# A convolution and attention block on one core: loads for the first image's Strassen sums issued earlier, and a division moved behind the last addition

## The chip, the cores and the metric

The kernel runs on one core of a Trainium2 chip. The metric is the device time of one execution in microseconds. The kernel before takes 2338.26 us, the median of three runs (2337.59 to 2338.87).

## The reference

Eight images of 512 channels and 32 x 32 pixels, all in float32. Each goes through a group norm, then through this block, and is added to the result:

```python
t = cbs(x, cv1_w, cv1_bn, 0)               # 1x1 convolution 512 -> 512, batch norm, silu
ys = [t[:, :C], t[:, C:]]                  # two halves of C = 256 channels
for i in range(N):                         # N = 2 bottlenecks
    yi = ys[-1]
    z = cbs(yi, m_cv1_w[i], m_cv1_bn[i], 1)                    # 3x3 convolution
    z = bot_attention(z, m_qkv_w[i], m_rw[i], m_rh[i])         # 4 heads of 64, 1024 positions
    z = jax.nn.silu(bn_eval(conv2d(z, m_cv2_w[i], 0), m_cv2_bn[i]))
    ys.append(yi + z)
return cbs(jnp.concatenate(ys, axis=1), cv2_w, cv2_bn, 0)      # 1x1 convolution 1024 -> 512
```

The attention takes q, k and v from a 1x1 convolution, adds a position term to k, and divides the exponentials of the scaled products by their sums.

## The kernel before, in words

**The stages of an image.** A Python loop over the eight images is unrolled. For each image: `conv3x3` of the first bottleneck (with the inputs transformed by `tiles_in` and the weights by `make_u`), `attention_fast`, the 1x1 convolution `m2` (L938), then the same again for the second bottleneck, then `cv2`. Parts of the next image's group norm and `cv1` and of this image's `cv2` are put inside the attention calls, to fill TensorE.

**Strassen.** From the second image on, `cv1` (L1084) and the projections q, k, v (L582, L586) are computed by Strassen's scheme on 2 x 2 blocks; `cv2` (L972) is for all images but the last. The scheme needs four sums of weight blocks each. They are made once, during the second attention of the first image, and put to DRAM, from which the later images load them: `make_ws` (for `cv2`), `make_sq(0)` and `make_sq(1)` (for the projections of the two bottlenecks) and `make_sw` (for `cv1`). `make_sw` first loads the weights of `cv1` as two halves of 512 KB (`w1_half`, L241, on SyncE's queue), makes the sums s1 to s4 on VectorE (L246 to L249) and stores them on GpSimd's queue (L251). `make_ws` finds its weights on the chip, and so does `make_sq`.

**Attention.** `attention_fast` walks over four groups: a group is a pair of heads and a half of the queries. A group has eight blocks of keys, taken in four pairs. For a pair, TensorE makes the products of q and k (L689), ScalarE takes the exponentials (L693, one for each block), VectorE adds them up in `acc` (L707 for the first pair, L709 otherwise), and TensorE multiplies them with v, one pair behind (L723). At a group's end ScalarE and VectorE bring the two halves of the result from PSUM to `ao` (L730, L731).

**The division.** TensorE sums `acc` over the partitions (`sums`, L741). The row of sums goes to DRAM (L748) and back in another shape (L778), VectorE takes the reciprocal (L785), and it goes to DRAM (L787) and comes back spread over the partitions as `rs` (L789). Then VectorE multiplies `ao` with it (`scale`, L797). The sums of group g are taken in group g + 1, its `rs` is made in the third pair of group g + 1, and its `scale` stands in the second pair of group g + 2. The last two groups are different. The fourth group's sums go a shorter way (`last_sums`, L759: two copies of the PSUM tile, an addition L834 and a reciprocal L835 on VectorE). The third group's `scale` is called at the end of `attention_fast`, between `last_sums` and L834.

**What orders the work.** The tile framework orders each engine's queue at compile time from the order of the program and from what it expects to be ready. `with tc.issue_after(ins)` puts the instructions of the block behind `ins` on its engine. A dictionary `behind` hands functions to `attention_fast`, which calls them at set places: -1 is behind the projections, g behind the first pair of v products of group g, (g, p) behind pair p of group g, `NG` = 4 behind the last pair, and `NG + 1` behind `last_sums`. All places but -1 are inside `issue_after(added.ins)`, where `added` is the latest addition to `acc`.

**The first image's second attention** has in `behind`: 0 `make_ws`, 1 the Strassen closures of `cv2` and the loads of the next transformed 3 x 3 weights (L332), 2 `make_sq(0)`, (2, 2) `make_sq(1)`, 3 `make_sw`, 4 the first product of `cv2` (`part1`: the sums `t1` on VectorE, L997, and 16 matmuls from the first image's `y` and `ypad`), 5 the second product (`part2`, from `t1`). That second product goes to the one PSUM buffer of tag `av`, which L731 frees.

**Buffers.** The `w1_half` tiles, the tiles of `make_sq` and the image tiles share the four buffers of tag `x`. The tiles of `make_sw` and the residual tiles `x_res` (loaded by GpSimd's queue, L1016) share the two of tag `xr`.

Of the kernel before, what the change touches and what calls it, by code (L numbers as in the profile page):

```python
# [61 lines left out]
def kernel(  # L62
# [47 lines left out]
    def ring(shape, name):  # L110
        return const.tile(shape, F32, tag="u", name=name, bufs=5)
# [6 lines left out]
    def load_w2(n=2):  # L118
        nk = (2 + N) * NM // 2
        ws = [ring([P, nk, C2], f"w2_{i}") for i in range(n)]  # L120
        for i, w in enumerate(ws):
            nc.sync.dma_start(w, cv2_w[ts(i, nk * P), :].rearrange("(k p) o -> p k o", p=P))
        return ws
# [90 lines left out]
    def block_qkv(n, o, i):  # L214
        return qkv_sb[:, n, i].rearrange("p (w c o) -> p c w o", w=3, c=NM)[:, o]
# [3 lines left out]
    def make_sq(n):  # L219
        (a11, a12), (a21, a22) = ([block_qkv(n, o, i) for i in range(2)] for o in range(2))  # L220
        parts = [act.tile([P, 2, 3, P], F32, tag="x", name="sq_new", bufs=NX) for _ in range(2)]
        s1, s2, s3, s4 = (t[:, j] for t in parts for j in range(2))
        nc.vector.tensor_tensor(s1, a21, a22, ALU.add)
        nc.vector.tensor_tensor(s2, s1, a11, ALU.subtract)
        nc.vector.tensor_tensor(s3, a11, a21, ALU.subtract)
        nc.vector.tensor_tensor(s4, a12, s2, ALU.subtract)
        for h, t in enumerate(parts):
            nc.gpsimd.dma_start(sq_dram[n][:, 2 * h : 2 * h + 2], t)
# [5 lines left out]

    sw_dram = tc.dram_tile([P, 4, NX // 2, C], F32, name="sw")

    def make_sw():
        halves = []
        for o in range(2):
            a = act.tile([P, NX, C], F32, tag="x", name="w1_half", bufs=NX)  # L240
            nc.sync.dma_start(a, cv1_w[:, ts(o, C)].rearrange("(k p) o -> p k o", p=P))  # L241
            halves.append((a[:, : NX // 2], a[:, NX // 2 :]))
        (a11, a12), (a21, a22) = halves
        parts = [act.tile([P, 2, NX // 2, C], F32, tag="xr", name="sw_new", bufs=2) for _ in range(2)]
        s1, s2, s3, s4 = (t[:, j] for t in parts for j in range(2))
        nc.vector.tensor_tensor(s1, a21, a22, ALU.add)  # L246
        nc.vector.tensor_tensor(s2, s1, a11, ALU.subtract)
        nc.vector.tensor_tensor(s3, a11, a21, ALU.subtract)
        nc.vector.tensor_tensor(s4, a12, s2, ALU.subtract)  # L249
        for h, t in enumerate(parts):  # L250
            nc.gpsimd.dma_start(sw_dram[:, 2 * h : 2 * h + 2], t)  # L251
# [78 lines left out]
    def load_u(n, oc, i):  # L330
        u = new_u("u")
        nc.sync.dma_start(u, u_dram[n][oc][i])  # L332
        return u
# [13 lines left out]
    def stages(act, small, ps_big, ps_av, n_pt):  # L347
# [316 lines left out]
        def attention_fast(n, z, at, behind, sq=None, mid=None):  # L664
# [13 lines left out]
            def logits(pair):  # L678
                g, j0 = pair[0]
                c, half = groups[g]  # L680
                pt = act.tile([P, PAIR, 2, HALF], F32, tag="pt", name="pt", bufs=n_pt)
                pts[pair[0]] = pt
                for i, (_, j) in enumerate(pair):
                    ps = ps_big.tile([P, 2, HALF], F32, tag="big", name="l_ps")
                    for hd in range(2):
                        r = slice(hd * HD, (hd + 1) * HD)
                        for kh in range(2):
                            o = j * P + kh * HD
                            nc.tensor.matmul(  # L689
                                ps[kh * HD : (kh + 1) * HD, hd, :], kr[r, c, o : o + HD],  # L690
                                q[r, c, ts(half, HALF)], start=True, stop=True,
                            )
                    exp = nc.scalar.activation(pt[:, i], ps, AF.Exp, scale=SCALE)  # L693
                if pair is pairs[-1]:
                    with tc.issue_after(exp.ins):
                        silu_in.append(table_of(AF.Silu))
                if j0 == 0 and g == 1 and later is not None:
                    accs[g] = None
                    return exp
                return add_up(pair)  # L700

            def add_up(pair):
                g, j0 = pair[0]
                pt = pts[pair[0]]
                if j0 == 0:
                    accs[g] = act.tile([P, 2, HALF], F32, tag="acc", name="acc", bufs=2)
                    return nc.vector.tensor_tensor(accs[g], pt[:, 0], pt[:, 1], ALU.add)  # L707
                for i in range(PAIR):
                    ins = nc.vector.tensor_tensor(accs[g], accs[g], pt[:, i], ALU.add)  # L709
                return ins  # L710
# [83 lines left out]
            def scale(g, rs):  # L794
                c, half = groups[g]
                dst = ao[:, c, ts(half, HALF)]
                nc.vector.tensor_tensor(dst, dst, rs, ALU.mult)  # L797
# [5 lines left out]
            s_drams, rss, evicted = {}, {}, [None]  # L803
            for i in range(len(pairs) + 1):
                if i < len(pairs):
                    added = logits(pairs[i])
                    g, at_q = divmod(i, NQ)
# [7 lines left out]
                if i > 0:  # L815
                    g, j0 = pairs[i - 1][0]
# [3 lines left out]
                    if i < len(pairs) and accs.get(pairs[i][0][0], 0) is None:  # L820
                        with tc.issue_after(evicted[0].ins):
                            added = add_up(pairs[i])
# [5 lines left out]
            g = len(groups) - 1  # L828
            ps, rows, s_dram = last_sums(g)
            with tc.issue_after(added.ins):  # L830
                behind.get(len(groups) + 1, lambda: None)()
            scale(g - 1, rss.pop(g - 1))
            rs = act.tile([P, HALF], F32, tag="rs", name="rs", bufs=2)
            nc.vector.tensor_tensor(rs, ps[:, 1, :], rows[0], ALU.add)  # L834
            nc.vector.reciprocal(rs, rs)  # L835
# [405 lines left out]
    for b in range(B):  # L1241
# [6 lines left out]
        def u_of(n):  # L1248
            def of(oc):
                nonlocal last_load  # L1250
                if b == 0 and oc == 1:
                    if n == 0:
                        with tc.issue_after(last.ins):
                            for i in range(PAIRS):
                                make(n, oc, [i])
                    else:
                        for k in range(NM):
                            raws[n, oc, k] = load_raw(n, oc, k, "kv"[k])
                        with tc.issue_after(last.ins):
                            make(n, oc, [1])  # L1260
                got = [us.pop((oc, i)) if (oc, i) in us else load_u(n, oc, i) for i in range(PAIRS)]
                if b > 0 and oc == 1:
                    sq[n], last_load = load_sq(n)
                return got

            return of
# [20 lines left out]
        def ahead():  # L1287
            nonlocal w1, sw
            g = next(groups)
            if g > 0 or b == 0:  # L1290
                next(norm, None)
            if g == 0:
                if b > 0:
                    for i in range(PAIRS):
                        us[0, i] = load_u(1, 0, i)
                w1 = load_w1() if more else load_w2(1)
                if more and b > 0:
                    sw = load_sw()
            if b == 0:
                if g == 0:  # L1300
                    raws[1, 1, 0], raws[1, 1, 1] = load_raws_y0(1, 1)
                    make(1, 1, [2])
                    del us[1, 2]
                elif g <= NM:
                    make(1, 1, [0], [g - 1])
# [22 lines left out]
        behind = {g: ahead for g in range(NG)} | {NG: first, NG + 1: second}  # L1328
# [16 lines left out]
        with tc.issue_after(last.ins):  # L1345
            check()
        z, mid = s.conv3x3(1, vs, u_of(1))
        w2 = ws = three = stored = None
        begun = {}
        if b == 0:  # L1350
            w2 = load_w2()

        def prepare():
            nonlocal stored, ws
            stored, ws = make_ws(w2)

        def ahead():
            nonlocal w2, three
            if more:
                three = s.strassen(b, ws or load_ws(), y0, y1)  # L1360
                for i in range(PAIRS):
                    us[0, i] = load_u(0, 0, i)
            else:
                w2 = load_w2()
# [10 lines left out]
        def second():  # L1375
            if more:
                three[1]()
            else:
                ks = range(2 * NM, (1 + N) * NM)
                begun[1] = ps_av.tile([P, NH, HALF], F32, tag="av", name="ps")  # L1380
                s.cv2_products(w2, (y0, y1, y2), 1, ks, begun[1], (ks[0], (2 + N) * NM - 1))

        behind = {1: ahead, NG: first, NG + 1: second}
        if b == 0:
            behind |= {0: prepare, 2: lambda: make_sq(0), (2, 2): lambda: make_sq(1), 3: make_sw}
        if six:
            behind |= {(1, 1): six[3], (2, 1): six[4]}
        ao, check = s.attention_fast(1, z, (b * N + 1) * NM * NH, behind, sq.get(1), mid)
# [29 lines left out]
    with tc.If(held < P):  # L1418
        with ExitStack() as gs:
# [6 lines left out]
            g = stages(g_act, g_small, g_big, g_av, 3)  # L1426
# [67 lines left out]
```

## Time and profile before

| | share of the span, or us |
|---|---|
| span of the profiled run | 2337.2 us |
| TensorE busy | 98% |
| VectorE busy | 78% |
| ScalarE busy | 42% |
| GpSimd busy | 4% |
| mean granted TensorE clock | 0.996 |
| DMA traffic, mean | 100 GB/s |

The page also gives the chain of work that ended last, followed back from the last instruction. It is TensorE for 93% of the span and VectorE for 4%. A busy TensorE in this profile includes the modelled ends of pipelined matmuls, so in the timelines the distance from one start to the next is the better measure: it is 0.43 us for a matmul of 128x128 by 512.

In a timeline, a row merges equal instructions of one engine. It has the start and the length in us, the engine, the line of the kernel, the operation, output and inputs, their shapes and the count. Brackets at the end give the idle time of the engine ahead of the row and what ended it. A name ending in q, as `SPq`, is the engine's queue of issues (DMA starts); the time of such a row is that of the issue, not of the transfer.

### The profile page before, as it was taken

The numbers are of one execution on the slowest core, as the hardware profiler recorded it, in microseconds if no ns is written. First come the engines' busy times: TensorE is split into PE (matmuls) and PEld (weight loads), VectorE is DVE, ScalarE is ACT, GpSimd is POOL, SyncE is SP. The second block draws the span as 40 slices with busy tenths as digits, with TensorE's granted clock in tenths as the row PEclk, the third lists the DMA queues.
The fourth block names the chain that finished last, engine by engine and source line by source line (L and its number), as shares of the span: only waits on it lengthen the run. The fifth ranks groups of instructions, "written<-read, shape, count | busy, mean of one in ns | idle before, by whom it ended". The sixth has DMA issues, their size and how long they took to land.

```text
span 2337.2 us, 36365 instructions
## 1 busy us (share of the span) xinstructions
PE 2298.2 (98%) x14746; PEld 1162.6 (50%) x14746; DVE 1826.2 (78%) x2899; ACT 980.2 (42%) x1282; POOL 88.9 (4%) x307
## 2 busy tenths in 40 slices
PE   7999989999999999999999999999999999999998
PEld 4536336363463635536364463645536364463643
DVE  8867767878778887888778877888877888777674
ACT  1442613536245362444525445253543535335352
POOL 1000000000000000000000000000000000000001
PEclk9999999999999999999999999999999999999999
DMA  7412326031240414304152131612216031250202
GB/s 255 154 54 90 109 78 230 15 131 48 94 193 15 149 33 142 143 15 149 34 200 89 47 113 51 240 36 78 82 46 247 29 120 40 65 219 16 86 11 70
DMA packets 95280, 234.80 MB, mean 100 GB/s; under 512 B 28032, under 2 KB 50496, under 8 KB 81664
## 3 DMA queue, kind: packets, MB, share of 16 engines
q1 hardware_dynamic: 83296, 182.05, 22.9%
q0 software_dynamic: 11808, 50.34, 5.6%
q8 instruction: 118, 1.93, 0.3%
q14 instruction: 58, 0.48, 0.1%
HBM read 197.75 MB, written 34.60 MB: 99 GB/s over the span
## 4 chain that ended last, share of the span: by engine, by line
PE 93%; DVE 4%; DMA 1%; ACT 1%; issue 0%; SPq 0%; POOL 0%; DVEq 0%; ACTq 0%
PE av_ps L723 18%; PE l_ps L689 18%; PE c_ps L917 14%; PE c L972 8%; PE p_ps L582 7%; PE x_ps L1084 6%; PE c_new L972 6%; PE m_ps L938 5%; PE ps L369 5%; PE pv_ps L586 3%; PE s_ps L741 1%; PE p_ps L586 1%; DVE acc L709 1%; PE s_ps L759 1%; PE v_ps L553 1%
## 5 line engine op out<-in xcount | busy, mean ns | idle before, releaser
L693 ACT ACTIVATE pt<-l_ps 128x1024 f32<-128x1024 f32 x512 | 494.9, 1023 | 408.4 <-PE l_ps L689 385.1
L709 DVE TENSOR_TENSOR acc<-acc,pt 128x1024 f32<-128x1024 f32 x384 | 469.4, 1222 | 65.8 <-ACT pt L693 42.5
L723 PE MATMUL av_ps<-pt,vT 64*64 64x512 f32 x4096 | 485.1, 591 | 1.1 <-DVE ao L731 1.1
L689 PE MATMUL l_ps<-q,kr 64*64 64x512 f32 x4096 | 484.2, 590 | 0.0
L917 PEld LDWEIGHTS c_ps<-v_in,u 128*128 128x128 f32 x2720 | 306.3, 192 | 8.0 <-issue 6.7
L917 PE MATMUL c_ps<-v_in,u 128*128 128x128 f32 x2720 | 306.9, 275 | 1.1 <-DVE v_in L426 1.1
L723 PEld LDWEIGHTS av_ps<-pt,vT 64*64 64x64 f32 x4096 | 152.0, 133 | 277.3 <-issue 230.7
L689 PEld LDWEIGHTS l_ps<-q,kr 64*64 64x64 f32 x4096 | 153.7, 133 | 269.7 <-issue 256.2
L433 ACT COPY m<-c_ps 128x256 f32<-128x256 f32 x96 | 35.4, 369 | 227.5 <-PE c_ps L917 222.5
L972 PE MATMUL c_new<-t_in,ws 128*128 128x512 f32 x288 | 124.6, 592 | 0.0
L938 PE MATMUL m_ps<-ao,m_sb 128*128 128x512 f32 x256 | 112.7, 593 | 0.0
L707 DVE TENSOR_TENSOR acc<-pt 128x1024 f32<-128x1024 f32 x64 | 78.1, 1220 | 25.8 <-ACT pt L693 25.8
L352 ACT ACTIVATE m_kept<-m_kept,bh,sh 128x512 f32<-128x512 f32 x42 | 31.9, 806 | 146.0 <-DVE m_kept L1056 86.3
L797 DVE TENSOR_TENSOR ao<-ao,rs 128x512 f32<-128x512 f32 x64 | 44.1, 689 | 60.4 <-DMA rs<-r_dram 59.8
L972 PEld LDWEIGHTS c_new<-t_in,ws 128*128 128x128 f32 x288 | 54.7, 190 | 68.9 <-issue 66.0
L352 ACT ACTIVATE t<-m_ps,bh,sh 128x512 f32<-128x512 f32 x64 | 48.0, 775 | 84.2 <-PE m_ps L938 82.7
L582 PE MATMUL p_ps<-t_z,sq 128*128 128x512 f32 x168 | 81.3, 593 | 0.0
L938 PEld LDWEIGHTS m_ps<-ao,m_sb 128*128 128x128 f32 x256 | 48.4, 190 | 61.7 <-issue 58.4
L946 DVE TENSOR_TENSOR ylast<-t,ypad 128x512 f32<-128x512 f32 x32 | 22.0, 692 | 66.5 <-ACT t L352 66.5
L352 ACT ACTIVATE z<-z,bh,sh 128x512 f32<-128x512 f32 x64 | 48.6, 806 | 50.9 <-DVE z L462 50.9
L426 DVE TENSOR_TENSOR v_in<-w_rows 128x512 f32<-128x512 f32 x96 | 65.9, 687 | 0.0
L972 PE MATMUL c<-ypad,ws 128*128 128x512 f32 x144 | 63.8, 592 | 0.0
(252 smaller groups left out, 2976.8 us busy)
## 6 DMA issues: line engine op xcount, KB each, us to landing
u<-u SPq DMA_DIRECT2D x85, 1024.0 KB
x<-in_x_dram SPq DMA_DIRECT2D x32, 512.0 KB
x_res<-in_x_dram POOLq DMA_DIRECT2D x28, 512.0 KB, 6.8
out_dram<-m_kept POOLq DMA_DIRECT2D x28, 512.0 KB, 7.3
w<-in_cv_w_dram SPq DMA_DIRECT2D x13, 1024.0 KB
u<-u_new POOLq DMA_DIRECT2D x12, 1024.0 KB, 5.6
rs<-r_dram SPq DMA_DIRECT2D x96, 128.0 KB
ws<-s SPq DMA_DIRECT2D x24, 512.0 KB
```

The lines of the kernel that those rows point to most:

```text
L352: return nc.scalar.activation(dst, src, AF.Silu, scale=sh[:, k : k + 1], bias=bh[:, k : k + 1])
L369: nc.tensor.matmul(ps[:, half, :], w_of(k), rhs_of(k, half), start=(k == begin), stop=(k == end))
L582: nc.tensor.matmul(ps[:, o, :], w[:, o, :], rhs, start=not onto, stop=True, skip_group_check=onto)
L586: nc.tensor.matmul(v[:, ts(j, P)], rhs[:, ts(j, P)], w[:, 2, :], start=j == 0 and not onto, stop=True, skip_group_check=True,)
L689: nc.tensor.matmul(ps[kh * HD : (kh + 1) * HD, hd, :], kr[r, c, o : o + HD], q[r, c, ts(half, HALF)], start=True, stop=True,)
L693: exp = nc.scalar.activation(pt[:, i], ps, AF.Exp, scale=SCALE)
L709: ins = nc.vector.tensor_tensor(accs[g], accs[g], pt[:, i], ALU.add)
L723: nc.tensor.matmul(avs[g][hd * HD : (hd + 1) * HD, kh, :], vT[r, j, o : o + HD], pt[r, i, hd, :], start=(j == 0), stop=(j == NJ - 1),)
L917: nc.tensor.matmul(ps[:, row, col, :], us[i][:, k, row, SLOT[col], :], vs[i][:, k, row, col, :], start=(k == 0), stop=(k == NM - 1),)
L938: nc.tensor.matmul(pss[oc][:, half, :], m2_sb[:, n, k, ts(oc, P)], ao[:, k, ts(half, HALF)], start=(k == 0), stop=(k == NM - 1),)
L972: nc.tensor.matmul(ps[:, o, :], w[:, k, ts(o, P)], rhs[part][:, c, :], start=(k == 0 and not onto), stop=(k == KB - 1), skip_group_check=onto,
L1084: nc.tensor.matmul(ps[:, o, :], w[:, c, ts(o, P)], rhs[c], start=(c == 0 and not onto), stop=(c == 1), skip_group_check=onto,)
```

## The change

It has three parts, all about the work that the first image's second attention does besides its own.

- `make_sw` is split. `load_halves` issues the two loads of `cv1`'s weights behind the projections of that attention (place -1), and `make_sw` makes the sums and stores them. It is called in the second group (place 1, in `ahead`) instead of the fourth (place 3).
- `make_sq(1)` moves from pair 2 of the third group, (2, 2), to the fourth group, 3, where `make_sw` was.
- In all 16 attention calls the third group's `scale` is put behind the last addition to `acc`, by an `issue_after`. Before, only the order of the program and its inputs bound it.

The first part is meant to have the loads behind the chip's other transfers and not among those of the division, the third to keep a division whose `rs` is late from holding up the last addition, on which `last_sums` waits.

```diff
-    def make_sw():
+    def load_halves():
         halves = []
         for o in range(2):
             a = act.tile([P, NX, C], F32, tag="x", name="w1_half", bufs=NX)
             nc.sync.dma_start(a, cv1_w[:, ts(o, C)].rearrange("(k p) o -> p k o", p=P))
             halves.append((a[:, : NX // 2], a[:, NX // 2 :]))
+        return halves
+
+    def make_sw(halves):
         (a11, a12), (a21, a22) = halves
...
             with tc.issue_after(added.ins):
                 behind.get(len(groups) + 1, lambda: None)()
-            scale(g - 1, rss.pop(g - 1))
+            with tc.issue_after(added.ins):
+                scale(g - 1, rss.pop(g - 1))
             rs = act.tile([P, HALF], F32, tag="rs", name="rs", bufs=2)
...
+        def load_ahead():
+            nonlocal halves
+            halves = load_halves()
+
...
         def ahead():
             nonlocal w2, three
+            if b == 0:
+                make_sw(halves)
             if more:
                 three = s.strassen(b, ws or load_ws(), y0, y1)
...
         if b == 0:
-            behind |= {0: prepare, 2: lambda: make_sq(0), (2, 2): lambda: make_sq(1), 3: make_sw}
+            behind |= {-1: load_ahead, 0: prepare, 2: lambda: make_sq(0), 3: lambda: make_sq(1)}
```

More of the change, by code (lines that the diff above doesn't have):

```diff
@@ L1347 @@
         z, mid = s.conv3x3(1, vs, u_of(1))
-        w2 = ws = three = stored = None
+        w2 = ws = three = stored = halves = None
         begun = {}
```

## The prediction

> **What bounds the kernel now.** I read the busy table first: TensorE is busy 98% of the span, and nothing else is near it. So a change to loads and VectorE adds can only win what TensorE loses by waiting, some 39 us in all, and the next view is the list of TensorE's waits (engine, line waited for, us in total, times, longest).
>
> ```profile
> PE 2298.2 (98%) x14746; PEld 1162.6 (50%) x14746; DVE 1826.2 (78%) x2899; ACT 980.2 (42%) x1282; POOL 88.9 (4%) x307
> ```
>
> ```profile
> PE gm_ps L475 <- DVE mv L470: 11.2, 1, 11.2
> PE s_ps L759 <- DVE acc L709: 5.1, 1, 5.1
> ...
> PE c L972 <- DVE ao L731: 1.9, 1, 1.9
> ```
>
> The first is the start of the kernel, which the change does not touch. The other two occur once each in 16 attention calls. The timeline of TensorE puts both in the first image's second attention; below it stands the same stretch of the second image.
>
> ```profile
> 291.19 3.70 PE L972 MATMUL c<-y,w 128*128 128x512 f32 x8
> 294.72 3.60 PE L972 MATMUL c<-ypad,w 128*128 128x512 f32 x8
> 303.43 1.98 PE L759 MATMUL s_ps<-acc,ones 64*64 64x512 f32 x8 [5.11 <-DVE acc L709]
> 307.35 9.00 PE L972 MATMUL c<-t_in,s 128*128 128x512 f32 x16 [1.93 <-DVE ao L731]
> ```
>
> ```profile
> 584.89 3.70 PE L972 MATMUL c<-y,ws 128*128 128x512 f32 x8
> 588.43 3.60 PE L972 MATMUL c<-ypad,ws 128*128 128x512 f32 x8
> 591.96 1.09 PE L759 MATMUL s_ps<-acc,ones 64*64 64x512 f32 x8
> 592.98 7.13 PE L972 MATMUL c<-t_in,ws 128*128 128x512 f32 x16
> 599.95 6.60 PE L938 MATMUL m_ps<-ao,m_sb 128*128 128x512 f32 x15
> ```
>
> From the first `c` to the first `m_ps` the second image takes 599.95 - 584.89 = 15.06 us. In the first image `m_ps` starts at 316.19, so the same 40 matmuls take 25.00 us. The excess, 9.94 us, is three things: `s_ps` starts 12.24 instead of 7.07 us after the first `c` (5.17), the next product 3.92 instead of 1.02 us after that (2.90), `m_ps` 8.84 instead of 6.97 us after that (1.87). The last term has no wait in it: after the hole the clock is halved. By windows the granted clock is 0.86 in 298 to 302, 0.50 in 302 to 306 and 0.57 in 306 to 312, about 10.3 us at half speed.
>
> Why `s_ps` is late is in VectorE's queue of that stretch:
>
> ```profile
> 282.96 0.68 DVE L797 TENSOR_TENSOR ao<-ao,rs 128x512 f32<-128x512 f32 x1
> 286.20 0.69 DVE L246 TENSOR_TENSOR sw_new<-w_half 128x512 f32<-128x512 f32 x1 [2.55 <-DMA w_half<-in_cv_w_dram]
> ...
> 291.20 0.20 DVE L785 RECIPROCAL rc<-sums_all 128x8 f32<-128x8 f32 x1
> 291.39 1.23 DVE L709 TENSOR_TENSOR acc<-acc,pt 128x1024 f32<-128x1024 f32 x1
> 301.46 0.69 DVE L797 TENSOR_TENSOR ao<-ao,rs 128x512 f32<-128x512 f32 x1 [8.84 <-DMA rs<-r_dram]
> 302.07 1.22 DVE L709 TENSOR_TENSOR acc<-acc,pt 128x1024 f32<-128x1024 f32 x1
> ```
>
> The third group's division (L797) stands ahead of the fourth group's last addition (L709), waits 8.84 us for `rs`, and the addition, the three sums of `t_in` and the PSUM addition L731 queue behind it. TensorE waits for the last L709, then for L731. `rs` itself is late, as the SyncE queue shows:
>
> ```profile
> 277.85 1.14 SPq L241 DMA_DIRECT2D w_half<-in_cv_w_dram x2
> 281.66 0.52 SPq L748 DMA_DIRECT2D s_dram<-s_row  x1
> 286.36 0.33 SPq L778 DMA_DIRECT2D sums_all<-s_dram  x1
> 291.43 0.34 SPq L787 DMA_DIRECT2D r_dram<-rc  x1
> 294.73 1.10 SPq L789 DMA_DIRECT2D rs<-r_dram  x2
> ```
>
> The tiny `s_dram` write holds L778 for 4.70 us behind the two halves of the weights (in the first group, at 252.03, it was 1.66). The reciprocal is late behind 2.55 us of wait for `w_half` and 2.54 us of its four sums (286.20 to 288.74), and the return of `rs` takes 3.30 us to issue and 6.73 more to arrive. In the second image these are 1.41 (581.06 to 582.47) and 3.58 (582.47 to 586.05). Meanwhile two residual loads of 512 KB go out on GpSimd's queue at 292.33 and 294.83, having waited for the sums' store.
>
> [...]
>
> **The change part by part.** *The loads.* Two loads of 512 KB go to behind the projections, about 230 us, or earlier, since the SyncE queue issues nothing between 211.34 and 252.03 and the DMA share is 0.00 from 220 to 230. Before they took at most 8.35 us (277.85 to 286.20), with other transfers beside them; so they are there by 240 and are needed near 254. Nothing waits for them, and they leave the stretch that matters. Cost 0.
>
> *The four sums in the second group.* 2.54 us of VectorE behind the second pair of group 1, near 254.2. VectorE there waits for ScalarE's exponentials 1.52 + 0.77 + 1.79 = 4.08 us up to 263.5, so the sums fit and 1.54 us is left. Behind them are that group's additions, which only release exponential buffers, and the first group's reciprocal, which moves from 258.2 to about 259.3; its `rs` comes by about 265, and its L797 stands at 268.5. Cost 0. Their stores and the residual loads, which wait for them, move 25 to 30 us earlier.
>
> *`make_sq(1)` in the fourth group.* Its four sums of 0.55 (2.0 us, 276.22 to 278.22) take the place of 2.55 + 2.54 = 5.09 us. L797 of group 1 ends at 283.6, the sums at 285.6, when the exponentials of the third pair are also ready. The third pair's additions end at 288.1, and the reciprocal comes there instead of at 291.20. The last pair's exponentials end near 289.0 (start 287.03, 1.94 us for two), so the last L709 ends near 290.8.
>
> *The division behind the last addition.* The last L709 now comes 12.5 us earlier than its end at 303.3. `s_ps` wants it at 298.2, so 7 us is left. Behind it come three `t_in` sums (3.4 us), L731 (0.6) and L797. `rs`: reciprocal 288.3, issue +1.4, arrival +3.6, so 293.3. From the other side, with this trace's disturbed 3.30 and 6.73, 298.3. I take 294, since the halves and residual loads are gone and only 768 KB of `sq` stores are in flight. L731 then ends by 296 (at worst about 300), and the product that needs it starts at 299.3. `m_ps` needs the division at 306.3. Both waits go, and with them the half clock: 25.00 becomes 15.06.
>
> *The other 15 attention calls.* All have L797 ahead of the last L709 and wait 2.9 to 4.1 us for `rs`, but TensorE never waits there, because 16 matmuls stand ahead of `s_ps`. The edit gives VectorE some slack that nobody uses. In six calls a weight load of `m_ps` waits for the last L797, 3.1 us in all, where 0.24 us of issue is normal, so at most 3.1 - 6 x 0.24 = 1.7 us. The 16 `m_ps` around one of them (467.13 to 474.00) run at the full 0.43 us each, so I take 0.
>
> Sum: 2338.26 - 9.94 = **2328.3 us**.
>
> **The rivals.** *The division becomes the new wait (0.13).* If `rs` is still as late as 301.46 and L797 stands ahead of L731, L731 ends at 302.8 and the product starts 3.5 us late. With about 3.4 us at half clock after it (1.7 lost) the gain is 9.94 - 5.2 = 4.7: 2333.5. For it: three large transfers still have to go somewhere. Against: they get 30 us of nearly idle DMA.
>
> *Nothing to be had (0.06).* VectorE falls behind in the second group, whose first pair already follows 5 us of `make_ws` sums (TensorE waits 0.63 us at 251.80 on L731), and exponentials stall; a stall of about 2.5 us on each of the three following groups eats 7.5 us: 2335.9. Against: the 4.08 us of waits.
>
> *Slower (0.06).* The division, now bound only from one side, is ordered behind the last reciprocal (L835, 3.35 us). In the six calls of images 1 to 6 before the first m2, `s_row` is there at 464.3, L834 and L835 run to 468.4, the division to 469.0, and `m_ps` wants it at 467.13: 1.9 us x 6 = 11.4 us, 2339.7. If every hole also halves the clock for 3.4 us (1.7 each), 2350. I put it at 2345. Against: `rs` is there by 459.3 and the chain to L834 is not, so the division is ready first.
>
> **How the numbers follow.** The full gain has 0.75: 2328.3. Low end: the 1.7 us of the weight loads besides, 2326.5. High end: the new wait with the noise of the runs (0.6), 2334.0. Outside are the two last rivals, 0.12, and some of the unforeseen. Faster by over 0.2% means under 2333.6: the full gain and most of the first rival, 0.86. Within: 0.08. Slower: 0.06.
>
> **What would show it.** TensorE's list of waits has neither `s_ps <- acc` nor `c <- ao L731`. The first `c` to the first `m_ps` of that attention takes 15 us at clock 1.00. L709 stands ahead of L797 in all 16 places, and the wait for `w_half` is gone. L778 follows L748 by 1.7 us in that group. The prediction is wrong if `m_ps` or `c` waits for L797 or L731, or if new holes appear near 250 to 285.

## The result, and the profile after

The changed kernel takes 2328.20 us, the median of four runs (2327.52 to 2328.51), against 2338.41 us for the kernel before. The ratio is 0.9956, with a 95% interval of 0.9939 to 0.9974. The prediction said 2328.3 us, in a range of 2326.5 to 2334.0. The gain of 10.2 us is 0.44%.

In the listings of this part, the change has moved the lines of the kernel: the last addition is now L712 (before L709), the reciprocal of a group L788 (L785), the division L800 (L797), the PSUM addition L734 (L731), `s_ps` L762 (L759), `c` L976 (L972), `m_ps` L942 (L938). In the kernels of the experiments a line can differ from these by one to three. The timeline of TensorE, for the same stretch as before:

```profile
289.61 3.70 PE L976 MATMUL c<-y,w 128*128 128x512 f32 x8
293.15 3.60 PE L976 MATMUL c<-ypad,w 128*128 128x512 f32 x8
296.68 1.09 PE L762 MATMUL s_ps<-acc,ones 64*64 64x512 f32 x8
297.69 7.13 PE L976 MATMUL c<-t_in,s 128*128 128x512 f32 x16
304.67 7.03 PE L942 MATMUL m_ps<-ao,m_sb 128*128 128x512 f32 x16
```

No row has a wait in brackets, and from the first `c` to `m_ps` it is 304.67 - 289.61 = 15.06 us, where it was 25.00. The granted clock is 1.00 in the windows 298 to 302, 302 to 306 and 306 to 312. TensorE's list of waits has neither `s_ps` behind `acc` nor `c` behind `ao` any more. Of what is left, the only wait on an addition in an attention's groups is

```profile
PE av_ps L726 <- DVE ao L734: 1.1, 2, 0.6
```

which stood there before, too. VectorE's queue in that stretch:

```profile
286.46 0.20 DVE L788 RECIPROCAL rc<-sums_all 128x8 f32<-128x8 f32 x1
286.64 2.55 DVE L712 TENSOR_TENSOR acc<-acc,pt 128x1024 f32<-128x1024 f32 x2
...
293.40 0.69 DVE L800 TENSOR_TENSOR ao<-ao,rs 128x512 f32<-128x512 f32 x1 [1.93 <-DMA rs<-r_dram]
294.01 1.22 DVE L1039 TENSOR_TENSOR t_in<-ypad,t_in 128x1024 f32<-128x1024 f32 x1
295.14 0.68 DVE L734 TENSOR_TENSOR ao<-av_ps,ao 128x512 f32<-128x512 f32 x1
```

Both last additions now stand ahead of the division. It still waits for `rs`, 1.93 us. The third sum of `t_in` and the PSUM addition are still behind it, and the PSUM addition ends at 295.8, 1.9 us before the product that needs it. The SyncE queue shows why `rs` is earlier:

```profile
182.07 2.09 SPq L241 DMA_DIRECT2D w_half<-in_cv_w_dram  x2
...
280.09 0.52 SPq L751 DMA_DIRECT2D s_dram<-s_row  x1
281.71 0.32 SPq L781 DMA_DIRECT2D sums_all<-s_dram  x1
286.68 0.33 SPq L790 DMA_DIRECT2D r_dram<-rc  x1
289.97 1.11 SPq L792 DMA_DIRECT2D rs<-r_dram  x2
```

The halves are loaded a whole stage earlier than the place in the program suggests, at 182 us. SyncE's queue had nothing else to issue between 163.6 and 182, and its list of waits has 18.4 us for these loads behind a matmul of L372, which reads an image tile. That fits a buffer of tag `x` that comes free there. L781 follows L751 by 1.62 us instead of 4.70.

The profiled spans differ by 11.0 us (2337.2 and 2326.2). It divides so. The first image's first `m_ps` starts 1.57 us earlier, which is chance and not the change (see the last section). The stretch above gives 9.94. From `m_ps` there to TensorE's last product it is 2327.45 - 316.19 = 2011.26 us before and 2315.67 - 304.67 = 2011.00 us now, so 0.26 more for all seven other images. From that product to the end of the program the changed kernel takes 0.78 us longer, 10.5 instead of 9.8; in the eight profiles of the experiments this end takes between 9.8 and 10.7 us, so it is not of the change either.

### The profile page after: what moved, and what is told of

Its sections match the earlier page's. It is cut to its first block, busy times and chain, and to the rows that moved or that the text cites. A ratio compares the mean times of both kernels' runs of the same rounds, so it can differ in the third digit from the quotient of the medians.

```text
span 2326.2 us, 36363 instructions
## 1 busy us (share of the span) xinstructions
PE 2293.7 (99%) x14746; PEld 1160.4 (50%) x14746; DVE 1827.8 (79%) x2899; ACT 980.6 (42%) x1282; POOL 88.9 (4%) x307
## 3 DMA queue, kind: packets, MB, share of 16 engines
q8 instruction: 118, 1.93, 0.3%
## 4 chain that ended last, share of the span: by engine, by line
PE 95%; DVE 3%; DMA 1%; ACT 0%; issue 0%; POOL 0%; SPq 0%; DVEq 0%; ACTq 0%
PE av_ps L726 19%; PE l_ps L692 19%; PE c_ps L921 14%; PE c L976 8%; PE p_ps L585 7%; PE x_ps L1088 6%; PE c_new L976 6%; PE m_ps L942 5%; PE ps L372 5%; PE pv_ps L589 3%; PE s_ps L744 1%; PE p_ps L589 1%; PE s_ps L762 1%; PE v_ps L556 1%; DVE acc L712 0%; DMA x_res<-in_x_dram 0%
## 5 line engine op out<-in xcount | busy, mean ns | idle before, releaser
L712 DVE TENSOR_TENSOR acc<-acc,pt 128x1024 f32<-128x1024 f32 x384 | 469.5, 1223 | 65.4 <-ACT pt L696 40.3
L976 PE MATMUL c_new<-t_in,ws 128*128 128x512 f32 x288 | 124.6, 592 | 0.0
L942 PE MATMUL m_ps<-ao,m_sb 128*128 128x512 f32 x256 | 112.5, 592 | 0.0
L976 PEld LDWEIGHTS c_new<-t_in,ws 128*128 128x128 f32 x288 | 54.7, 190 | 68.9 <-issue 66.0
L942 PEld LDWEIGHTS m_ps<-ao,m_sb 128*128 128x128 f32 x256 | 48.6, 190 | 61.2 <-issue 61.2
L976 PE MATMUL c<-ypad,ws 128*128 128x512 f32 x144 | 63.8, 592 | 0.0
L1088 PE MATMUL x_ps<-t_x,sw 128*128 128x512 f32 x144 | 62.8, 592 | 0.0
```

Source lines behind the costliest of these rows:

```text
L942: nc.tensor.matmul(pss[oc][:, half, :], m2_sb[:, n, k, ts(oc, P)], ao[:, k, ts(half, HALF)], start=(k == 0), stop=(k == NM - 1),)
L976: nc.tensor.matmul(ps[:, o, :], w[:, k, ts(o, P)], rhs[part][:, c, :], start=(k == 0 and not onto), stop=(k == KB - 1), skip_group_check=onto,
L1088: nc.tensor.matmul(ps[:, o, :], w[:, c, ts(o, P)], rhs[c], start=(c == 0 and not onto), stop=(c == 1), skip_group_check=onto,)
```

## The experiments

Two theories were to be told apart. By mine, TensorE loses what it does because of the place of the division in VectorE's queue together with the arrival of `rs`. The division must be past, or must stand behind, the last addition when TensorE reaches `s_ps`, and the PSUM addition when it reaches the second product. By the rivals one part alone is the cause: the loads, or the order. The table gives the results, from the profiles in us after the first `c`, which itself starts between 289.6 and 291.6. Each median is of the runs of that kernel: five, but four of the changed kernel, 21 of the division alone and ten of the loads alone. The first four columns of numbers are from one profile each. The kernel before was 2338.44 beside the first four and 2339.04 beside the last four.

| kernel | division starts | `s_ps` | second product | `m_ps` | median us | ratio to before (95%) |
|---|---|---|---|---|---|---|
| before | 10.27 | 12.24 | 16.16 | 25.00 | 2338.41 | |
| changed | 3.79 | 7.07 | 8.08 | 15.06 | 2328.20 | 0.9956 (0.9939 to 0.9974) |
| moves alone | 3.17 | 7.07 | 9.06 | 16.03 | 2329.63 | 0.9961 (0.9948 to 0.9975) |
| division alone | 10.41 | 7.07 | 12.89 | 21.56 | 2335.52 | 0.9987 (0.9980 to 0.9994) |
| loads alone | 5.95 | 7.93 | 11.84 | 20.51 | 2333.65 | 0.9979 (0.9970 to 0.9989) |
| loads and division | 5.40 | 7.07 | 8.09 | 15.06 | 2328.74 | 0.9957 (0.9943 to 0.9971) |
| division in one place | 3.67 | 7.07 | 8.09 | 15.06 | 2328.70 | 0.9956 (0.9943 to 0.9970) |
| projection sums back | 2.48 | 7.06 | 8.08 | 15.05 | 2327.88 | 0.9957 (0.9943 to 0.9970) |
| division behind the PSUM addition | 11.28 | 7.07 | 8.09 | 15.06 | 2328.15 | 0.9956 (0.9942 to 0.9970) |
| division behind the reciprocal | 13.32 | 7.06 | 8.08 | 15.05 | 2329.30 | 0.9960 (0.9946 to 0.9974) |

**Moves alone.** The changed kernel without its `issue_after` around the division:

```diff
-            with tc.issue_after(added.ins):
-                scale(g - 1, rss.pop(g - 1))
+            scale(g - 1, rss.pop(g - 1))
```

> The loads and sums are moved as in the changed kernel, the division is bound as before, so it stands ahead of the last addition again. Times are counted from the first c of the first image's second attention. Theory (the place of the division in VectorE's queue and the arrival of rs together set the loss): rs comes at 3.8 us as in the changed kernel, so the last addition ends at 5.6, in time for s_ps at 7.1; but three t_in sums and the PSUM addition still follow it, to 9.6, and the product that needs the PSUM buffer waits 1.5 us instead of starting at 8.1. m_ps at 16.6 at full clock: 2329.7 us[...]. Rival (the moved loads are the whole cause): no wait, m_ps at 15.1, 2328.2 us.

VectorE's queue and, below it, TensorE's timeline of this kernel:

```profile
293.86 0.69 DVE L800 TENSOR_TENSOR ao<-ao,rs 128x512 f32<-128x512 f32 x1 [4.91 <-DMA rs<-r_dram]
294.47 1.22 DVE L712 TENSOR_TENSOR acc<-acc,pt 128x1024 f32<-128x1024 f32 x1
...
299.01 0.68 DVE L734 TENSOR_TENSOR ao<-av_ps,ao 128x512 f32<-128x512 f32 x1
```

```profile
299.75 7.13 PE L975 MATMUL c<-t_in,s 128*128 128x512 f32 x16 [0.90 <-DVE ao L734]
```

The last addition is behind the division again, but `rs` comes 7.1 us earlier than before (3.17 against 10.27), so `s_ps` does not wait. What is left is 0.98 us at the second product, with no half clock behind it (the 16 matmuls take 306.72 - 299.75 = 6.97 us). I had expected 1.5; `rs` came 0.6 us earlier than I had put it. The moves alone bring nine tenths of the stretch's gain: 25.00 - 16.03 = 8.97 of 9.94.

**Division alone.** The kernel before with only the `issue_after`.

```diff
-            scale(g - 1, rss.pop(g - 1))
+            with tc.issue_after(added.ins):
+                scale(g - 1, rss.pop(g - 1))
```

> The kernel before with the division bound behind the last addition and nothing else. Theory: rs comes at 10.3 us after the first c as before; the last addition ends at 2.6, s_ps starts at 7.1 without a wait, but the division stands ahead of the third t_in sum and of the PSUM addition, which ends at 12.7, so the product starts 4.6 us late, and with about 3.4 us of half clock behind the hole m_ps comes at 21.4 instead of 25.0: 2334.7 us. Rival (the order of division and addition is the whole cause): no wait, 2328.3 us.

Again VectorE and TensorE:

```profile
302.02 0.69 DVE L797 TENSOR_TENSOR ao<-ao,rs 128x512 f32<-128x512 f32 x1 [5.38 <-DMA rs<-r_dram]
...
303.76 0.68 DVE L731 TENSOR_TENSOR ao<-av_ps,ao 128x512 f32<-128x512 f32 x1
```

```profile
304.50 8.83 PE L973 MATMUL c<-t_in,s 128*128 128x512 f32 x16 [4.73 <-DVE ao L731]
```

The wait at `s_ps` is gone and one for L731 has taken its place, 4.73 us. The 16 matmuls behind it take 313.17 - 304.50 = 8.67 us instead of 6.97, and the clock is 0.59 from 305 to 309, which is 3.3 us at half speed. For the 3.4 us at half clock in the prediction and in the expectation there is a measured stretch in the trace of the kernel before: 3.41 us at clock 0.50, from 65.39 to 68.80. This is the first rival of the prediction, which had put a late `rs` at 3.5 us of wait and 1.7 of clock. It is what the edit does without the moves: 3.44 us of 9.94 in this profile, 2.9 us by the medians (2338.44 and 2335.52).

**Loads alone.** From the changed kernel, the division as before, and the sums at their old places:

```diff
-                make_sw(halves)
...
-            behind |= {-1: load_ahead, 0: prepare, 2: lambda: make_sq(0), 3: lambda: make_sq(1)}
+            behind |= {-1: load_ahead, 0: prepare, 2: lambda: make_sq(0), (2, 2): lambda: make_sq(1), 3: lambda: make_sw(halves)}
```

> Only the loads of the two weight halves are moved ahead; their sums stay in the fourth group, the projection sums in the third, and the division stands ahead of the last addition. Theory: the wait of 2.6 us for the halves is gone and the reciprocal comes at -2.6 us from the first c instead of 0, but the store of the sums and the residual loads behind it are still among the transfers of rs, which comes at about 7.1 us; then s_ps waits 1.9 us, the product starts at 13 instead of 16.2 and m_ps at about 21.7: 2335 us. Rival (the halves' loads alone delay rs): rs at 3.8 us as in the changed kernel, 2329.7 us.

TensorE's timeline:

```profile
298.24 1.09 PE L762 MATMUL s_ps<-acc,ones 64*64 64x512 f32 x8 [0.79 <-DVE acc L712]
302.15 8.83 PE L975 MATMUL c<-t_in,s 128*128 128x512 f32 x16 [2.83 <-DVE ao L734]
```

`rs` is 4.3 us earlier than before (5.95 against 10.27), which is 2.64 from the earlier reciprocal (-2.63 instead of 0.01) and 1.7 from a shorter way through DRAM (8.58 us from the reciprocal's start to the division, instead of 10.26). In the kernel with the sums moved too it came at 3.17. So the loads are the larger part of the delay and the place of the sums another 2.8 us: 0.5 of it from a still earlier reciprocal, 2.26 from the way through DRAM (6.32 instead of 8.58), beside which the stores of the sums and the residual loads no longer lie. I had put `rs` at 7.1; the direction held, and the loss was smaller by the 1.1 us.

**Loads and division.** The kernel just told, with the division bound as in the changed kernel:

```diff
-            scale(g - 1, rss.pop(g - 1))
+            with tc.issue_after(added.ins):
+                scale(g - 1, rss.pop(g - 1))
```

> The loads are moved ahead and the division is bound behind the last addition; the sums stay in the fourth group, so their store and the residual loads stay among the transfers of rs. Theory: rs at about 7.1 us after the first c; no wait at s_ps; the division runs to 7.7, the third t_in sum and the PSUM addition to 9.5, and the product waits 1.4 us: 2329.7 us[...]. Rival (with the loads ahead and the division bound the place of the sums does not matter): 2328.2 us.

```profile
296.68 0.69 DVE L800 TENSOR_TENSOR ao<-ao,rs 128x512 f32<-128x512 f32 x1 [3.00 <-DMA rs<-r_dram]
...
298.42 0.68 DVE L734 TENSOR_TENSOR ao<-av_ps,ao 128x512 f32<-128x512 f32 x1
```

In VectorE's queue the PSUM addition ends at 299.1, 7.8 us after the first `c`, and the product starts at 8.1. The wait that I expected missed by a quarter of a microsecond, because `rs` came at 5.4 and not at 7.1. So the rival's number is right. With the loads ahead and the division bound, where the sums are made no longer decides anything, but the slack is 0.27 us, where the changed kernel has 1.9.

**The division in one place.** The changed kernel with the edit left in the first image's second attention alone:

```diff
-            with tc.issue_after(added.ins):
+            with tc.issue_after(added.ins) if at == NM * NH else nullcontext():
                 scale(g - 1, rss.pop(g - 1))
```

> The changed kernel with the division bound behind the last addition in the first image's second attention alone; the 15 other calls keep the order of before. Theory (TensorE never waits in the other 15): m_ps 15.1 us after the first c, 2328.2 us. Rival (the edit also gains in the other calls, as the 1.7 us of waiting weight loads): 2329.9 us.

The stretch is the same, and the medians differ by 0.5 us, which these runs cannot tell from nothing. In the profiles the other seven images, from the first image's second `m_ps` to the last product, take 2317.63 - 305.83 = 2011.80 us here and 2011.00 in the changed kernel. The same stretch takes 2011.26 to 2011.80 us in the four profiles without the binding in those calls (the kernel before, moves alone, loads alone, and this one), and 2010.99 to 2011.00 in the five that have it there. (The division behind the reciprocal is left out; it is told of below.) So the rival is right in kind: the edit brings 0.26 to 0.80 us in the other calls. The difference lies at `m_ps` of the first attentions of the second to the seventh image. With the binding the 16 products take 6.87 us from start to start in each of them. Here they take up to 7.22:

```profile
1024.53 7.39 PE L942 MATMUL m_ps<-ao,m_sb 128*128 128x512 f32 x16
```

In those calls a weight load of `m_ps` waits for the division, 4.2 us in six waits here and not at all in the changed kernel, and a part of it comes through to the matmuls.

**The projection sums back** in the third group, the rest as in the changed kernel:

```diff
-            behind |= {-1: load_ahead, 0: prepare, 2: lambda: make_sq(0), 3: lambda: make_sq(1)}
+            behind |= {-1: load_ahead, 0: prepare, 2: lambda: make_sq(0), (2, 2): lambda: make_sq(1)}
```

> The changed kernel with the second projection sums back in the third group. Theory: VectorE has room there too, their store no longer lies beside rs, which comes at about 2.5 instead of 3.8 us after the first c; TensorE sees nothing of it: 2328.2 us. Rival (the third group has no room, exponentials stall): some 2 us more, 2330.2 us.

`rs` comes at 2.48 us, as expected, and TensorE sees nothing of it. But the store is not the main reason. Of the 1.31 us, 0.91 is the reciprocal, which starts 4.06 us ahead of the first `c` and not 3.15, since these sums no longer stand ahead of it in VectorE's queue. The way through DRAM is only 0.40 us shorter (6.54 against 6.94), and in the kernel with the moves alone, which has the store where the changed kernel has it, it was 6.32. What the store costs is not shown. This part of the change costs 1.3 us of `rs` and brings nothing.

**The division behind the PSUM addition.** The kernel before, with no load moved:

```diff
-            scale(g - 1, rss.pop(g - 1))
+            with tc.issue_after(evicted[0].ins):
+                scale(g - 1, rss.pop(g - 1))
```

> The kernel before, loads and sums where they were, with the division bound one step further, behind the PSUM addition of the fourth group, in all 16 calls. Theory: rs still comes 10.3 us after the first c, but only the division waits for it: the last addition ends at 2.8, the PSUM addition at 6.8, the product starts at 8.1, the division ends at 11.1, m_ps starts at 15.1 at full clock: 2328.5 us, the whole gain without moving a load. Rival (the transfers must move, since the division then delays the last reciprocal and with it the second half of m_ps, which TensorE reaches at 18.5): the last division ends at 15.9 by the theory; if it came after 18.5 there would be a wait again and the time would be above 2330 us.

VectorE's queue:

```profile
296.94 0.68 DVE L731 TENSOR_TENSOR ao<-av_ps,ao 128x512 f32<-128x512 f32 x1
301.76 0.69 DVE L797 TENSOR_TENSOR ao<-ao,rs 128x512 f32<-128x512 f32 x1 [4.14 <-DMA rs<-r_dram]
...
306.47 0.69 DVE L797 TENSOR_TENSOR ao<-ao,rs 128x512 f32<-128x512 f32 x1
```

`rs` is later than in the kernel before, at 11.28 us, and it costs TensorE nothing: 15.06 us from the first `c` to `m_ps`, and a median of 2328.15 us. The last division (the fourth group's, the last row) ends at 16.7, and TensorE reaches the half of `m_ps` that needs it at 18.5, so 1.8 us are left. This is the strongest test of the theory. The whole gain is had by order, with the division bound behind the PSUM addition and not only behind the last addition to `acc`, and all transfers left as they were.

**The division behind the reciprocal.** The order of the slower rival of the prediction:

```diff
-            with tc.issue_after(added.ins):
-                scale(g - 1, rss.pop(g - 1))
...
-            nc.vector.reciprocal(rs, rs)
+            made = nc.vector.reciprocal(rs, rs)
+            with tc.issue_after(made.ins):
+                scale(g - 1, rss.pop(g - 1))
```

> The changed kernel with the division bound behind the last reciprocal in all 16 calls, the order that the slower rival of the prediction was about. Theory: in the six first attentions of images 1 to 6 the division ends at about 1.9 us after TensorE reaches m_ps, in the last attention of all 2.5 us after it, in the nine others before it: 6 x 1.9 + 2.5 = 13.9 us above the changed kernel, 2342.1 us[...]. Rival (a late division is hidden everywhere): 2328.2 us.

This was a clear miss: 2329.30 us instead of 2342.1. TensorE's timeline of the second image's first attention shows why:

```profile
457.44 1.88 PE L942 MATMUL m_ps<-ao,m_sb 128*128 128x512 f32 x4
459.16 1.11 PE L1088 MATMUL x_ps<-t_x,sw 128*128 128x512 f32 x2
460.11 5.31 PE L942 MATMUL m_ps<-ao,m_sb 128*128 128x512 f32 x12
```

In the kernels before and after, the 16 `m_ps` are one block. In the changed kernel it is

```profile
455.61 7.03 PE L942 MATMUL m_ps<-ao,m_sb 128*128 128x512 f32 x16
```

Here TensorE's queue, which the framework orders anew for each kernel, has four of them first and two matmuls of the next image's `cv1` behind them, and the other twelve start 2.67 us after the first. The 1.9 us of hole that were expected are filled: from the first attention's `m_ps` of an image to the second's, each of the six images takes 132.91 us instead of 132.82. Only in the last attention, where there is no next image, a wait is left, 0.51 us instead of 2.5:

```profile
2292.69 5.42 PE L942 MATMUL m_ps<-ao,m_sb 128*128 128x512 f32 x12 [0.51 <-DVE ao L800]
```

## Why the prediction was right

**The number.** The measured median is 2328.20 us and the predicted one 2328.3. The mechanism was right, but agreement to 0.1 us is luck: the runs of the changed kernel spread over 1.0 us, and in the two profiles chance differences of 1.57 and -0.78 us stand beside the change.

**The stretch.** It said that the two waits and the half clock behind them are one loss of 9.94 us, and that all of it goes. The profile has 15.06 us, as the second image had. The other five kernels in which both additions are done in time have the same within 0.01.

**VectorE's times.** Counted from the first `c`, the reciprocal was put at -3.1 and stands at -3.15; the end of the last addition at -0.4 and it is -0.42. The sums in the second group cost TensorE nothing, and neither do the second projection sums in the fourth: its list of waits has no new entry. So the rival by which there is nothing to be had did not come either. One detail was wrong. The prediction named three sums of `t_in`, L731 and L797 in this order behind the last addition, but the division stands ahead of the third sum and of the PSUM addition, which ends 6.2 us after the first `c` where the prediction had 4.8.

**The arrival of `rs`** was put too early. The prediction took 2.8 us after the first `c`, and it was 3.79. The way from the end of the reciprocal was put at 1.4 + 3.6 us, and 0.7 more for the stores in flight; it was 3.29 (286.68 to 289.97) + 3.43. So the mis-sized term is "issue +1.4". Its cause stays open. With the projection sums back in the third group it is 1.41, but it is 1.40 in the kernel with the moves alone too, where their store lies beside it as here; in both of these the second step is longer instead, 4.91 and 4.70. The range for `rs` reached to 7.1, and the slack at the product was 1.9 us, so nothing came of it.

The 4.70 against 1.66 us of the small write are from one queue, since the halves and the write both go out on SyncE's; with the halves loaded earlier it was 1.62. For transfers from two queues there are the loads alone: beside stores and loads from GpSimd's queue the way of `rs` on SyncE's takes 8.58 us, and 6.32 in the kernel with the moves alone, where the sums' stores and the residual loads lie elsewhere. What makes it longer is not shown.

**The other 15 calls** were put at 0, with 1.7 us as the bound. They gave 0.26 us by the two profiles, and up to 0.80 by the others (see the division in one place). VectorE's wait for `rs` fell from 59.8 us in 16 places to 7.8 in 4, and the 3.1 us of weight loads waiting for the division are gone. Nearly none of it was on TensorE's path, but not none: the prediction took 0 from one call in which the 16 `m_ps` run at full speed, but in two others of the six they take 6.93 and 7.02 us in the kernel before, instead of 6.87.

**The rivals.** The first was right in its mechanism, and the kernel with the division alone is that case: a product 4.8 us late where the prediction had 3.5, and 1.7 of clock as it had it. It had left out the third sum of `t_in`, 1.1 us, which stands between the division and the PSUM addition. The slower one was wrong. Its step "the division is at 469.0, and `m_ps` wants it at 467.13" held the order of TensorE fixed while it changed that of VectorE. With the queue as the framework then orders it, the late division costs 1.1 us by the medians and 1.3 by the profiles (2012.30 against 2011.00 us for the other seven images).

**What each part is worth.** The parts overlap. Of the 9.94 us, the moves alone bring 8.97 and the binding alone 3.44, in one profile each; loads and binding bring all, and so does a binding behind the PSUM addition with no moves. So the moves need the binding for the last tenth only, and the binding as the change has it needs the early loads. Moving the second projection sums was not needed.

## What to carry to other kernels

A small operation that waits for a long way through DRAM should stand in its engine's queue behind everything that another engine waits for, and not only behind the first of these: here that alone gave the whole gain, with no transfer moved. It holds as long as the small operation itself is still in time for whoever needs it. Price a hole on TensorE with the clock behind it: here 1.70 us were lost at half clock behind a wait of 4.73 us, and none behind one of 0.90. And when an order is changed on one engine, look at what the framework then does with the others, before counting a hole that they may fill.

## What the runs showed that I had not expected

**Behind 3.6 us of holes in two parts there was as much half clock as behind one hole of 4.73.** Behind the hole of 4.73 us (division alone) the clock is 0.59 over the 4 us from 305, and behind two holes of 0.79 and 2.83 us (loads alone) 0.66 over the 5 us from 302: 3.3 and 3.4 us at half speed, each costing the 16 matmuls 1.70 us (8.67 instead of 6.97). In the kernel before, with holes of 5.11 and 1.93, it was 10.24 us, from 300.91 to 311.15, three times that. The hole of 0.90 us (moves alone) cost none.

**The same short holes cost half clock in nine profiles and not in the tenth.** Near 62 to 65 us all kernels have two waits of 1.26 and 1.21 us. By the window from 60 to 80 us the clock is 0.91 in the profiles of the kernel before and of all eight experiments, and 1.00 in that of the changed kernel alone. The 52 matmuls there take 7.70 us before and 6.07 in the changed kernel. The change does not touch that place, and the eight kernels with its parts do not have it, so this 1.6 us of the two profiles' difference is chance.

In the trace of the kernel before the clock is 0.50 from 65.39 to 68.80 us and from 300.91 to 311.15, and 1.00 in all the rest from 22 to 2327 us. In the trace of the changed kernel it is 1.00 from 24 to 2315 us. What decided between the two near 65 us is not shown. The 21 runs of the division alone spread over 5.0 us, and the ten of the loads alone over 3.3; only one run of each has a trace, so it is not shown whether the clock makes that spread.
